# Masking by TensorE in the last attention steps of a two-layer network, with a new order of the work

## The chip, the core and the metric

The kernel runs on one core of a Trainium2 chip. Its time is the device time of one execution in microseconds. Before the change three runs took 934.36, 934.62 and 934.98 us, with a median of 934.62.

The core has five engines, each with its own queue that runs in order: TensorE (PE; its weight loads are listed apart as PEld), VectorE (DVE), ScalarE (ACT), GpSimd (POOL) and SyncE (SP, which starts DMAs here).

## The reference

`x` has 16 batches of 256 rows of 128 features. Everything is fp32.

```python
x = x + 0.5 * L0_ffn(layernorm(x))      # first feed-forward
x = x + L0_attn(layernorm(x))           # linear attention, no softmax
x = x + 0.5 * L0_ffn(layernorm(x))      # second feed-forward, the same weights
x = x + 0.5 * L1_ffn(layernorm(x))      # low-rank experts, 2 of 8 for each batch
x = x + L1_attn(layernorm(x))           # 16 heads of 8, rotary, causal softmax
x = x + 0.5 * L1_ffn(layernorm(x))      # the experts again

# L0_ffn: h = silu(x W1) * (x W2); h = gelu(h H1); h = gelu(h H2); out = h W3   (128 -> 512 -> 512 -> 512 -> 128)
# L1_attn:
scores = einsum('bhqd,bhkd->bhqk', q, k) / sqrt(8)
scores = where(causal, scores, -inf)
attn = softmax(scores, axis=-1)
out = einsum('bhqk,bhkd->bhqd', attn, v)
```

## The kernel before

**Groups and steps.** The 16 batches go in nine groups, seven of two batches (512 rows) and two of one (256 rows). Groups count from 0 to 8, batches from 0 to 15, so groups 7 and 8 are batches 14 and 15. Each group goes through `ffn` twice, 18 times in all. Between the two stands `nonlocal_attn`; after the second come `experts`, `attention` and `after_attention`, which also writes the output.

**A planner writes the order.** Each piece of work is a Python generator, a "line", that yields steps. A step names its engine, an assumed time, how many PSUM banks it takes, which buffers it takes and gives back, and what it needs. The loop at the end of the function always issues the step that the planner's own clocks say can start first; among steps that can start within `SLACK`, it prefers by a key. The line `main` runs the feed-forwards. `HURRY` says how many feed-forwards at the end are preferred to other lines; `PATIENCE` delays an exp when another activation table is loaded; `LOAN` makes the four low banks dearer for short uses; `LATE` is the number of last groups whose attention goes in halves. Assumed times only shape the order. The chip then runs each queue as it was written, with semaphores between engines. Nearly every instruction is recorded by one helper, so the profile gives them all as L227, and tiles tell them apart:

- `xnT`: normalised rows turned round, the input of `w1T` and `w2T`; `sil`: silu of the first product; `h`: hidden rows; `T` and `hS`: sums for a seven-product scheme of the two hidden layers; `w3s`: the last linear's weights
- `qkv`: masked and rotated queries and keys; `mx`: maxima of scores; `pr`: probabilities; `vm`: values; `den`, `rec`, `inv`, `oT`: denominators, their inverses and the scaled output; `wo`: the output projection
- `ab`: an expert's gathered weights; `we`: the merged expert of a batch
- `pb`: the eight PSUM banks

**Attention of one batch.** `maxima` computes scores with queries along the partitions, masks them and reduces them to a maximum for each query and head. Variant 0 and variant 1 are two sets of heads. The negated maxima are turned round (`ident,mx`) and put into spare rows of the queries (`qm`). `weighted` then computes the scores again, transposed, in four quarters `j` in the order 0, 2, 1, 3, each of which takes four banks; `softmax` takes exp of a quarter on ACT, and POOL sets the weights of later keys to zero on the two diagonal blocks, one `affine_select` each. `values` multiplies a quarter by `vm`. In the last `LATE` groups the two variants go one after the other through maxima, quarters, output and a projection each; in the earlier groups they go together.

**Masks.** The flag `ended` is set when the last feed-forward has been issued. From then on the scores of `maxima` are masked by TensorE, which adds `tri` (bf16, from `causal`, -1e30 at later keys) through a bf16 identity `eye` into the bank ahead of the scores; both lie in the tile `wgT`. Before, DVE adds `causal`. From `ended` on, `awake` also issues matmuls of `ident` with `ident` into a free bank wherever the planner sees TensorE idle.

**TensorE's modes.** Most matmuls use the whole array. Scores use four row tiles of 32 x 128 (`tiles="row"`), values four column tiles of 128 x 32 (`tiles="col"`).

Of the kernel before, what the change touches and what calls it, by code (L numbers as in the profile page):

```python
# [20 lines left out]
P = 128  # L21
# [7 lines left out]
LOAN = 1.5  # L29
SPARED = 0.5  # L30
PATIENCE = 1.5
HURRY = 1
# [11 lines left out]
LATE = 2  # L44
SPLIT = 0
HID = 512
KC = HID // P
# [10 lines left out]
def macaron_kernel(ctx: ExitStack, tc: tile.TileContext, a: dict, out: bass.AP):  # L58
# [316 lines left out]
    def ffn(which, t0, n):  # L375
# [79 lines left out]
        for c in range(KC):  # L455
            r = yield pe(0.215 * n, banks=1, after=0.0, take=("h",) if c == 0 else ())
            h = r[1] if c == 0 else h
            pu = r[0]
            nc.tensor.matmul(pu.t[:, :N], w1T[:, c * P : (c + 1) * P], xnT.t[:, :N], start=True, stop=True)
            sil = sml.tile([P, TG], F32, name="sil", bufs=3)  # L460
            spawn(silu(c, pu, sil))
            (pw,) = yield pe(0.215 * n, banks=1, after=0.0, drop=(xnT,) if c == KC - 1 else ())
            nc.tensor.matmul(pw.t[:, :N], w2T[:, c * P : (c + 1) * P], xnT.t[:, :N], start=True, stop=True)
            spawn(product(c, pw, sil, h))
            if me == (0, 0) and c == 1:
                fold_w3()
        lo, hi = 0, 2 * P
        for l, w in ((1, h1T), (2, h2T)):
# [9 lines left out]
            for p, b, first, at, second, needs in (  # L478
# [9 lines left out]
                for o in range(2):  # L488
                    for k in range(2):
                        begins, ends = o + k == 0, o + k == 2  # L490
                        drop = ()
                        if ends and p in (5, 7, 4):
                            drop = (T[{5: 1, 7: 3, 4: 4}[p]],) + ((h,) if p == 4 else ())
                        r = yield pe(
                            0.1075 * n, banks=int(new and begins), after=0.0, take=("h",) if p == 1 and begins else (),
                            needs=needs, drop=drop, sets=(("P6", l, me),) if p == 6 and ends else (),
                        )
                        if new and begins:
                            bk[b] = r[0]
                        if p == 1 and begins:  # L500
                            nh = r[1]
                        src = block(h, *second) if type(second) is tuple else T[second].t[:, :, :M]
                        nc.tensor.matmul(
                            in_two(bk[b])[:, o, :], first[:, k, at + o * P : at + o * P + P], src[:, k, :],
                            start=new and begins, stop=p in (2, 3, 4, 6) and k == 1, skip_group_check=True,
                        )
# [12 lines left out]
            h = nh  # L519

        half = n // 2
        po = {}
        up, down = (0, 1, 2, 3), (2, 3, 0, 1)
        for t, ks in [(t, down) for t in range(half, n)] + [(t, up) for t in range(half)]:
            new = t in (0, half)
            last = t in (half - 1, n - 1)
            r = yield pe(
                0.225 * len(ks), banks=int(new), after=0.0, needs=tuple((2, i, t // half, me) for i in range(2)),
                drop=(h,) if t == half - 1 else (),
            )  # L530
            if new:
                po[t // half] = r[0]
            b = po[t // half]
            for k in ks:
                nc.tensor.matmul(
                    b.t[:, t % half * P : (t % half + 1) * P], h.t[:, k, t * P : (t + 1) * P], w3s[:, k, :],
                    start=(k == ks[0]), stop=(k == ks[-1]),
                )
            if last:
                spawn(residual(t // half, b))  # L540
# [11 lines left out]
    def nonlocal_attn(t0, n):  # L552
# [20 lines left out]
        gram = yield from product(0.45 * nb, None, None, "gram", (xn,))  # L573
        m = yield from product(0.22 * nb, gram, pht, "gph")
        m = yield from product(0.22 * nb, m, wgT, "eff")
        if t0 == 2 * FIRST[NG - 1]:
            spawn(for_the_mask())
        (po,) = yield pe(0.45 * nb, banks=1, drop=(xnT,))
# [8 lines left out]
    def gated(nb, cls):  # L587

        (bk,) = yield pe(0.22 * nb, banks=1)
# [35 lines left out]
        (bk,) = yield pe(0.23 * nb, banks=1, drop=(ab,))  # L625
# [12 lines left out]
    def applied(key, sg, xnT):  # L638
        yield step(None, 0.0, needs=(key,))
        we = merged[key]  # L640
        (po,) = yield pe(0.225 * sg.n, banks=1, drop=(we, xnT) if sg.last else (xnT,))
# [61 lines left out]
    def attention(sg):  # L703
# [6 lines left out]
        if sg.first:  # L710

            (bk,) = yield pe(0.22 * nb, banks=1)
# [35 lines left out]
        (bk,) = yield pe(0.225 * n, banks=1, needs=(("q", sg.t0),), drop=(xnT,))  # L748
# [76 lines left out]
        def weighted(i):  # L825
# [10 lines left out]
            def softmax(j, q, pr):  # L836

                yield act(4 * o - 96, table="exp", drop=(q,))
                nc.scalar.activation(pr[:, :, :o], q.t[:, :, :o], AF.Exp)
                yield step("POOL", 0.65 * sum(k == f for k, f, _ in runs), sets=(("pr", sg.t0, i, j),))  # L840
# [40 lines left out]
            def values():  # L881

                po = [None, None]
                for j in (0, 2, 1, 3):
                    new = j == 0 or (late and j == 1)
                    yield step(None, 0.0, needs=(("pr", sg.t0, i, j), ("v", sg.t0)))
                    pr = prs[j]
                    r = yield pe(0.025 + 0.00174 * o, banks=int(new), tiles="col", drop=(pr,))
                    if new:
                        po[j % 2 :] = [r[0]] * (2 - j % 2)  # L890
                    half = slice((j % 2) * w, (j % 2) * w + w)
                    pp = po[j % 2].t[:, half]
                    for k, f, at in runs:
                        for r in range(4):
                            nc.tensor.matmul(
                                pp[32 * r : 32 * r + 32, (f - q0) * P :], vm.t[:, base // P + k, r, j, :],
                                pr.t[:, r, at : at + (q1 - f) * P],
                                start=(j < 2 and k == 0), stop=(j >= 2 and k == q1 - 1), skip_group_check=True,
                            )
                    if late and j >= 2:  # L900
                        spawn(output(pp, oT[:, half], w // 32, j % 2, po[j % 2], ("oT", sg.t0, i, j)))
                    elif j == 3:
                        spawn(output(po[0].t[:, : 2 * w], oT[:, : 2 * w], w // 16, 0, po[0], ("oT", sg.t0, i, j)))
# [3 lines left out]
            for j in (0, 2, 1, 3):  # L907
                q, prs[j] = yield pe(
                    0.11 + 0.00174 * o, banks=4, tiles="row", take=("pr",), needs=(("qm", sg.t0, i, j % 2),), after=0.0
                )  # L910
                for k, f, at in runs:
                    for r in range(4):
# [3 lines left out]
                            qm[rows, j % 2, base + f * P : base + q1 * P], start=True, stop=True,  # L916
                        )
                spawn(softmax(j, q, prs[j].t))
# [189 lines left out]
    def feed_forwards():  # L1108

        for which, sg in order:  # L1110
# [13 lines left out]
            if (which, sg) == order[0]:  # L1124
                fold_rest()
        ended[0] = True
# [10 lines left out]
    while lines:  # L1137
# [5 lines left out]
        line = min(soon, key=lambda r: ((r[2] is main) == back, r[2].rank, r[1]))[2]  # L1143
# [72 lines left out]
```

## Time and profile before

| | us |
|---|---|
| median of the runs | 934.62 |
| the profiled execution | 934.55 |
| its span, first to last instruction | 932.8 |
| TensorE busy | 904.2 |
| VectorE busy | 636.3 |
| ScalarE busy | 471.5, of which table loads (86 in the group, 1283 ns each) 110.3 |
| GpSimd busy | 356.4, of which 128 selects of `pr` 78.8 |

The span is 1.75 us shorter than the time of the same execution. "Busy" is the time in which an engine runs at least one instruction. Matmuls overlap, so a group's mean duration is longer than the distance between the starts of two neighbours; the prediction goes by starts. A row of the timeline gives start, duration, engine, line, operation, tile written and tiles read, form and count, and, in brackets, how long the engine was idle before and what ended that. A row of the windows gives start and end, length, then the busy time and count of PE, PEld, DVE, ACT and POOL, the granted share of TensorE's clock, the DMA share and GB/s.

### The profile page before, as it was taken

What the parts mean: (1) busy time and instruction counts of PE and PEld (TensorE: products, weight loads), DVE (VectorE), ACT (ScalarE), POOL (GpSimd) and SP (SyncE); (2) the same over time, 40 slices, a digit from 0 to 9 for tenths busy, and PEclk for the clock granted to TensorE, in tenths of its full rate; (3) what the DMA queues carried; (4) which work ended last, traced back from release to release, by engine and by line L of the source; (5) the groups of instructions that cost most, each with busy time, mean ns of one, the idle gap of its engine ahead of it and who ended that gap; (6) DMA issues with size and microseconds to landing.
All of it is one profiled execution on the core that took longest, in us unless ns stands there. A gap on an engine that the chain in (4) does not pass through costs nothing.

```text
span 932.8 us, 16458 instructions
## 1 busy us (share of the span) xinstructions
PE 904.2 (97%) x6524; PEld 680.5 (73%) x6524; DVE 636.3 (68%) x1474; ACT 471.5 (51%) x691; POOL 356.4 (38%) x537
## 2 busy tenths in 40 slices
PE   6999999999999999999999999999999989999998
PEld 4778778686786767787677767866786767877666
DVE  4744646875488485894678764894778586977773
ACT  2233533645754646546555466547574657465332
POOL 5311313522454334442453324532463246443441
PEclk9999999999999999999999999999999999999999
DMA  8100000000000000000000000000000000000000
GB/s 240 33 1 1 1 1 12 12 1 1 13 12 12 1 2 12 24 1 1 12 1 24 1 1 13 24 1 1 13 2 23 1 12 1 25 7 2 13 19 12
DMA packets 14588, 13.68 MB, mean 15 GB/s; under 512 B 2032, under 2 KB 11952, under 8 KB 14512
## 3 DMA queue, kind: packets, MB, share of 16 engines
q1 hardware_dynamic: 12496, 8.04, 3.0%
q0 software_dynamic: 1600, 4.20, 1.6%
q8 instruction: 51, 0.84, 0.4%
q10 hardware_dynamic: 416, 0.39, 0.1%
q14 instruction: 25, 0.20, 0.1%
HBM read 10.53 MB, written 2.10 MB: 14 GB/s over the span
## 4 chain that ended last, share of the span: by engine, by line
PE 70%; DVE 14%; ACT 6%; issue 4%; POOL 2%; DMA 2%; SPq 1%; POOLq 0%; DVEq 0%
PE pb L227 70%; DVE mx L227 4%; DVE h L227 3%; ACT L227 2%; ACT pr L227 2%; DVE pb L227 2%; DMA w3s<-in_w3T_dram 1%; ACT h L227 1%; POOL pr L227 1%; DVE T L227 1%; DMA x<-in_x_dram 1%; DVE st L227 1%; DVE qkv L227 1%; POOL rstd L227 1%; DVE row L227 0%
## 5 line engine op out<-in xcount | busy, mean ns | idle before, releaser
L227 DVE TENSOR_TENSOR h<-h,pb 128x512 f32<-128x512 f32 (+1 forms) x180 | 111.7, 620 | 80.8 <-PE pb L227 78.8
L227 PE MATMUL pb<-T,hS 128*128 128x256 f32 (+1 forms) x576 | 131.8, 364 | 3.9 <-DVE h L227 2.8
L227 POOL TENSOR_SCALAR_AFFINE_SELECT pr<-pr 128x512 f32<-128x512 f32 x128 | 78.8, 639 | 140.4 <-ACT pr L227 135.3
L227 ACT ACTIVATE h<-h 128x512 f32<-128x512 f32 (+1 forms) x108 | 62.3, 581 | 137.7 <-DVE h L227 137.3
L227 ACT ACTIVATE pr<-pb 128x1536 f32<-128x1536 f32 x64 | 92.7, 1449 | 54.0 <-PE pb L227 40.4
L227 PE MATMUL pb<-qkv 32*128 32x256 f32 (+2 forms) x1536 | 115.2, 406 | 4.7 <-ACT pr L227 2.5
L227 ACT ACT_TABLE_LOAD x86 | 110.3, 1283 | 17.8 <-PE pb L227 15.5
L227 DVE TENSOR_REDUCE mx<-pb 128x8 f32<-128x2048 f32 (+1 forms) x64 | 111.9, 1750 | 6.1 <-PE pb L227 5.7
L227 PEld LDWEIGHTS pb<-T,hS 128*128 128x128 f32 x576 | 96.5, 190 | 21.1 <-issue 8.6
L227 DVE TENSOR_TENSOR pb<-pb,causal 128x1024 f32<-128x1024 f32 x56 | 68.7, 1226 | 45.4 <-PE pb L227 37.3
L227 PEld LDWEIGHTS pb<-qkv 32*128 32x128 f32 x1536 | 68.0, 184 | 38.3 <-issue 11.4
L227 ACT ACTIVATE xn<-x,shift,rstd 128x128 f32<-128x128 f32 x138 | 57.1, 482 | 52.9 <-POOL shift L227 52.7
L227 POOL TENSOR_SCALAR nm<-mv 128x4 f32<-128x4 f32 (+3 forms) x56 | 14.8, 264 | 168.3 <-DVE mv L227 167.1
L227 POOL TENSOR_TENSOR T<-h 128x512 f32<-128x512 f32 (+1 forms) x48 | 53.4, 1112 | 58.9 <-ACT h L227 54.9
L227 POOL TENSOR_TENSOR T<-h,T 128x512 f32<-128x512 f32 (+1 forms) x40 | 46.1, 1151 | 64.9 <-DVE h L227 35.0
L227 PE MATMUL pb<-xnT,w1T 128*128 128x512 f32 (+1 forms) x144 | 68.9, 560 | 0.9 <-ACT xnT L227 0.9
L227 PE MATMUL pb<-xnT,w2T 128*128 128x512 f32 (+1 forms) x144 | 68.2, 555 | 1.0 <-ACT sil L227 0.8
L227 PE MATMUL pb<-h,h1T 128*128 128x256 f32 (+1 forms) x288 | 68.8, 364 | 0.0
L227 POOL TENSOR_TENSOR rstd<-ve,mhalf 128x4 f32<-128x4 f32 (+3 forms) x63 | 58.9, 935 | 24.9 <-DVE ve L227 20.1
L227 PE MATMUL pb<-h,h2T 128*128 128x256 f32 (+1 forms) x288 | 67.1, 364 | 0.0
L227 PE MATMUL pb<-T,h1T 128*128 128x256 f32 (+1 forms) x288 | 66.1, 359 | 0.0
L227 PEld LDWEIGHTS pb<-w3s,h 128*128 128x128 f32 x512 | 60.6, 192 | 7.0 <-issue 6.0
(138 smaller groups left out, 1568.9 us busy)
## 6 DMA issues: line engine op xcount, KB each, us to landing
out_dram<-x SPq DMA_DIRECT2D x7, 256.0 KB, 2.3
x<-in_x_dram SPq DMA_DIRECT2D x6, 256.0 KB, 5.3
h1T<-in_h1T_dram SPq DMA_DIRECT2D x1, 1024.0 KB, 9.6
h2T<-in_h2T_dram SPq DMA_DIRECT2D x1, 1024.0 KB, 11.0
ab<-in_eab_dram,at POOLq DMA_INDIRECT x32, 2.9
x<-in_x_dram SPq DMA_DIRECT2D x3, 128.0 KB, 5.4
w1T<-in_w1T_dram SPq DMA_DIRECT2D x1, 256.0 KB, 3.5
w2T<-in_w2T_dram ACTq DMA_DIRECT2D x1, 256.0 KB, 3.9
```

The costliest lines, as they stand in the source:

```text
L227: return lambda *args, **kw: tc.keep_in_program_order(getattr(self.engine, name)(*args, **kw))
```

## The change

1. **Planner constants.** `LOAN` 1.5 to 1.0, `PATIENCE` 1.5 to 1, `HURRY` 1 to 0, `LATE` 2 to 3. The assumed times of many TensorE steps grow by 0.015 us or about 5%.
2. **Last linear.** The part of `ffn` that multiplies by `w3s` becomes a generator of its own, spawned as a line. `main` ends the feed-forwards with a step that needs the last feed-forward's two residuals, and sets `ended` after it.
3. **Mask of the transposed scores.** In `weighted`, where `ended` is set, eight bf16 matmuls (`tri` as the stationary operand, `eye` moving, 128 columns) put the mask into the diagonal blocks of a quarter ahead of its scores; `softmax` then issues no select for it.
4. **Values.** Where a group isn't in the last `LATE`, two quarters (0 and 2, then 1 and 3) go in one step.
5. **Choice among ready steps.** While TensorE is in a tile mode, a ready step with tiles goes ahead of one without.

```diff
-LOAN = 1.5
+LOAN = 1.0
...
-PATIENCE = 1.5
-HURRY = 1
+PATIENCE = 1
+HURRY = 0
...
-LATE = 2
+LATE = 3
...
-            r = yield pe(0.215 * n, banks=1, after=0.0, take=("h",) if c == 0 else ())
+            r = yield pe(0.015 + 0.215 * n, banks=1, after=0.0, take=("h",) if c == 0 else ())
...
-        half = n // 2
-        po = {}
...
+        def last_linear(h=h):
+
+            half = n // 2
+            po = {}
...
+                if last:
+                    spawn(residual(t // half, b))
+
+        spawn(last_linear(), since=0.0)
...
-            def softmax(j, q, pr):
-
-                yield act(4 * o - 96, table="exp", drop=(q,))
+            def softmax(j, q, pr, masked):
+
+                yield act(4 * o - 96, table="exp", drop=(q,), sets=(("pr", sg.t0, i, j),) if masked else ())
                 nc.scalar.activation(pr[:, :, :o], q.t[:, :, :o], AF.Exp)
+                if masked:
+                    return
                 yield step("POOL", 0.65 * sum(k == f for k, f, _ in runs), sets=(("pr", sg.t0, i, j),))
...
-                for j in (0, 2, 1, 3):
-                    new = j == 0 or (late and j == 1)
-                    yield step(None, 0.0, needs=(("pr", sg.t0, i, j), ("v", sg.t0)))
...
+                for js in ((0,), (2,), (1,), (3,)) if late else ((0, 2), (1, 3)):
+                    new = js[0] == 0 or (late and js[0] == 1)
+                    yield step(None, 0.0, needs=tuple(("pr", sg.t0, i, j) for j in js) + (("v", sg.t0),))
+                    r = yield pe(
+                        (0.025 + 0.00174 * o) * len(js), banks=int(new), tiles="col", drop=tuple(prs[j] for j in js)
+                    )
...
+                masked = ended[0]
                 q, prs[j] = yield pe(
-                    0.11 + 0.00174 * o, banks=4, tiles="row", take=("pr",), needs=(("qm", sg.t0, i, j % 2),), after=0.0
+                    0.11 + 0.00174 * o + (0.75 if masked else 0.0), banks=4, tiles="row", take=("pr",),
+                    needs=(("qm", sg.t0, i, j % 2),), after=0.0,
                 )
+                if masked:
+                    diagonal = [at for k, f, at in runs if k == f]
+                    for r in range(4):
+                        for at in diagonal:
+                            nc.tensor.matmul(
+                                q.t[:, r, at : at + P], tri, eye, start=at == diagonal[0], stop=False, skip_group_check=True
+                            )
...
+        yield step(None, 0.0, needs=tuple(("ffn", h, (1, order[-1][1].t0)) for h in range(2)))
         ended[0] = True
...
         back = engine == "PE" and begun[0] <= len(order) - HURRY
-        line = min(soon, key=lambda r: ((r[2] is main) == back, r[2].rank, r[1]))[2]
+        inside = engine == "PE" and tiles[0] is not None
+        line = min(
+            soon, key=lambda r: (inside and r[2].next["tiles"] is None, (r[2] is main) == back, r[2].rank, r[1])
+        )[2]
```

## The prediction

> **What bounds the kernel now.** First the page's busy times, then the same by stretch of the span.
>
> ```profile
> span 932.8 us, 16458 instructions
> PE 904.2 (97%) x6524; PEld 680.5 (73%) x6524; DVE 636.3 (68%) x1474; ACT 471.5 (51%) x691; POOL 356.4 (38%) x537
> ```
>
> ```profile
> 400.00:500.00 100.00, 99.82 (x722) 74.45 (x720) 68.01 (x144) 54.12 (x72) 38.35 (x53) 1.00 0.03 9
> 750.00:800.00 50.00, 45.86 (x423) 36.30 (x421) 39.46 (x113) 31.08 (x48) 28.42 (x44) 1.00 0.03 8
> 850.00:875.00 25.00, 23.45 (x259) 17.11 (x260) 19.71 (x52) 9.59 (x14) 10.33 (x16) 1.00 0.04 12
> 875.00:900.00 25.00, 23.61 (x254) 16.80 (x252) 21.52 (x62) 8.50 (x11) 10.91 (x17) 1.00 0.06 17
> 900.00:933.00 33.00, 26.21 (x267) 19.42 (x264) 14.38 (x35) 6.95 (x7) 6.33 (x10) 0.94 0.03 9
> ```
>
> From about 30 to 600 us TensorE all but never stops: what is put on it or taken from it there is paid in full. After 850 its busy time deceives. Of the 100 matmuls of `ident` with `ident`, 90 are fillers that `awake` puts there; at 0.22 us each 19.8 us of the last 83 are no work. The end is a chain of latencies, read from the timeline:
>
> ```profile
> 843.47 2.05 PE L227 MATMUL pb<-w3s,h 128*128 128x128 f32 x16
> 869.08 0.60 PE L227 MATMUL pb<-wgT 128*128 128x256 bf16 x4
> 895.48 0.61 PE L227 MATMUL pb<-wgT 128*128 128x256 bf16 x4
> ```
>
> The last linear of the last feed-forward ends at 845.4. Batch 14 starts its first masked score at 869.1, batch 15 at 895.4, the end is 932.8: sections A, B, C of 23.7, 26.3 and 37.4, together 87.4 us. [...]
>
> **The change part by part.** A host planner writes the order, so new cost constants reorder everything. I took counts from the built order of both kernels and priced them by the trace.
>
> *Mode changes.* [...]
>
> ```profile
> 809.57 1.95 PE L227 MATMUL pb<-T,hS 128*128 128x128 f32 x16
> 811.35 0.83 PE L227 MATMUL pb<-h,h2T 128*128 128x128 f32 x6
> 834.99 1.95 PE L227 MATMUL pb<-T,hS 128*128 128x128 f32 x16
> 836.87 0.94 PE L227 MATMUL pb<-qkv 32*128 32x256 f32 x16
> ```
>
> Sixteen equal passes took 1.78 us ahead of the same mode and 1.88 ahead of row tiles. Over all starts of the trace the median pass of 128 columns is 112 ns, and 205 ahead of another mode; of 256 columns 216 and 309. One change costs 93 ns. The two-quarter step and the preference for tile lines take them from 378 to 332: 46 x 0.093 = 4.3 us less. The Trainium skill ("TensorEngine Tiling (Array Packing)", Key Properties) says that a change of mode drains the array, without a price; its fixed part of an isolated warm matmul, 166 ns ("TensorE: Matmul & The Clock Gate", Single matmul latency), would make 7.6 us by estimate. The row decides: 4.3.
>
> *Work added.* `LATE` 3 sends the two batches of group 6 the split way: 4 more transposes of maxima and 4 more projections by `wo`, 8 x 0.22 = 1.8 us of TensorE; on DVE 4 halves of den, rec, inv and oT in place of 2 wholes, (4 x 1.56) - (2 x 2.42) = 1.4 us, hidden under TensorE. The masks are 64 bf16 matmuls of 128 columns, each with a weight load. The trace has only 256 columns, at 108 ns from start to start.
>
> ```profile
> L227 PEld LDWEIGHTS <-wgT 128*128 128x128 bf16 x32 | 3.1, 97 | 1.8 <-issue 1.5
> ```
>
> Half of 108 is 54, the load alone 97, both in turn 151. I take 97, the time of the one part that the trace shows in just this form: 6.2 us (3.5 to 9.7). All stand after the last linear, where they partly replace fillers (90 to 63, -5.9 us).
>
> *Work removed.* Only 16 of 128 selects go, those of batches 14 and 15; group 6 keeps its own. A pair costs 1.22 us on POOL between exp and values.
>
> *Table loads.* The smaller `PATIENCE` lets exp cut in sooner: 87 loads become 111.
>
> ```profile
> 839.32 1.45 ACT L227 ACTIVATE pr<-pb 128x1536 f32<-128x1536 f32 x1
> 840.79 1.28 ACT L227 ACT_TABLE_LOAD   x1
> 842.08 0.38 ACT L227 ACTIVATE h<-pb 128x256 f32<-128x256 f32 x1
> ```
>
> Exp ends at 840.77, the load runs 840.79 to 842.07, the next activation starts 0.01 later: 1.28 us all told, 24 x 1.283 = 30.8 us more ACT, from 51% to 54% busy. The skill speaks harder against the change here ("ScalarE: Activation LUTs", What ACT_TABLE_LOAD costs): a drain of about 1.38 us comes with each load, 2.66 in all. That would be 63.8 us, and ACT at 57%. The rows show no such drain; I take 30.8, hidden while TensorE has other lines to run. Uncovered, every microsecond is paid: the first rival below.
>
> *What moves.* With `HURRY` 0 the feed-forward yields to every other ready line to its very end; the last linear, now its own line, may also use the low banks. In the built order the work of TensorE ahead of the last `w3s` matmul, fillers and changes left out, priced at 429, 216 and 112 ns a pass (two passes for fp32, tiles four at a time), grows from 756.2 to 764.4 us. Behind it, it falls from 37.1 to 30.7. Ahead there are 31 changes fewer (2.8 us). The last linear therefore ends 8.2 - 2.8 = 5.4 us later if the idle time ahead stays: 850.8. That is a choice. Between the end of the third last linear (742.0) and of the last (845.2) there are 103.2 us for 88.0 of work, so 15.2 idle; after there are 95.3 of work. Idle of 5 (all but the hops filled) to 26 (as thinly covered as ACT's new loads allow) bounds it: -10 to +11 us.
>
> *Section A, 23.7 to 8.6.* The queries of batch 14 come before or just behind the last linear, no longer 13 us later. The way to its first masked score runs along ACT: from 0.5 us ahead of the linear's end a table load 1.28, three remaining exps 3 x 1.45, between them y 0.49, keys and query 4 x 0.59, xnT 0.37, then a hop of 0.1: -0.5 + 1.28 + 4.35 + 3.2 + 0.1 = 8.4, taken as 8.6. Before, six exps lay behind the linear, each with a select.
>
> *Section B, 26.3 to 31.4.* With batch 14's first masked score as zero: scores and reduces of the first variant end at 7.2 (1.9, 2.29, 1.5, 1.22, hops), the second variant's large reduce at 12.8. The masks of the first quarter wait for the bank that `we` of batch 15 reads last, 10.5; exp ends 13.5. Second quarter: masks, scores 14.1 to 15.8, exp to 17.4. Values, transposes and the expert product of batch 15: 18.2. Its residual, norm, POOL's rstd 0.72 and xn: 21.6. Third exp ends 22.5, fourth quarter's masks and scores 24.1, its exp 25.75, its values 26.6. Only behind them stand `wqk` of batch 15 (27.6); rotary on DVE and POOL, and the last query 3.8 more. This order costs 5.1 us.
>
> *Section C, 37.4 to 35.3.* What it is now:
>
> ```profile
> 918.76 1.45 ACT L227 ACTIVATE pr<-pb 128x1536 f32<-128x1536 f32 x1 [1.26 <-PE pb L227]
> 920.28 1.22 POOL L227 TENSOR_SCALAR_AFFINE_SELECT pr<-pr 128x512 f32<-128x512 f32 x2 [1.49 <-ACT pr L227]
> 921.28 0.59 PEld L227 LDWEIGHTS pb<-pr,vm 128*32 128x32 f32 x16
> ```
>
> The last values start 25.9 after the section's start. Afterwards: first quarter's masks 8 x 0.097 on the way, exp at 11.2 in place of 10.2; second quarter ready when that exp ends (12.6), its exp to 16.4, values 17.4; third masks and scores 19.1, exp 20.8; the fourth's last four masks wait for that exp, scores 22.1, exp 22.3 to 23.7, values at 23.8. The select and its hop are gone (1.3), three masks lie on the path, an earlier second quarter makes up for them: -2.1. The rest, 11.5 us, is unchanged.
>
> *Sum.* 8.6 + 31.4 + 35.3 = 75.3 against 87.4: -12.1. With +5.4: 932.8 - 6.7 = 926.1 span. The profiled run took 934.55, 1.75 around its span: 927.9. The median before, 934.62, is 0.07 above: **928.0 us**. If masks cost 54 or 151, some 40 on the path shift it by about -2 or +2.
>
> **The rivals.**
>
> *ACT starves the feed-forward (slower).* One of the loads added is between silu and exp in the last feed-forward, where TensorE has few other lines; in the stretch to the last linear ACT's sum by the trace's means goes from 36 us to 50, beside 63 of TensorE, 13 loads in place of 9. If each of the four more costs its load and the exp that it brings, 4 x (1.28 + 1.45) = 10.9 us of idle TensorE: 938.9. Against it: ACT's waits for DVE (137.3 us for h) show slack all along, and no wait of matmuls on sil passes 1 us now. It decides from 6.7 us, 22% of the 30.8.
>
> *The shorter end is eaten (no change).* DVE is busy 41.2 of 50 us from 850 to 900. If A and B are DVE's, the end shrinks by just the 5.4 that moved ahead: 934.6. For it: reduces of 2.29 us. Against it: 17 us less DVE work by the means lies behind the last linear.
>
> *The idle time ahead is filled (faster).* `HURRY` 0 exists in the order: attention matmuls stand between those of the last feed-forward. If 8 of 15.2 idle go: 920.0.
>
> **How the numbers follow.** My forecast 0.55, own range 922 to 932; filled idle 0.17; eaten 0.10; starved 0.18. The bound of 0.2% (1.9 us) is what a measurement can tell from no change: faster 0.55 + 0.17 = 0.72, same 0.10, slower 0.18. The range 917 to 940 reaches from below the filled case to above the starved one, with the masks' two ends.
>
> **What would show it.** Right: last `w3s` pass ending near 851; batch 14's first mask some 9 us later, batch 15's 31 after that; values following exp by 0.1 us; a pass ahead of a mode change still 93 ns longer, 46 fewer. Wrong: the linear's end past 858 with matmuls waiting on sil or ACT h; section A over 15 us; mask pairs above 151 ns; gaps of TensorE between 100 and 600 us, where there are none now.

## The result: 0.8% slower, and the profile after

The kernel after takes 941.59 us (median, 939.11 to 944.07) against 934.36 of the kernel before, a ratio of 1.0076 with an interval of 1.0059 to 1.0093. The forecast was 928.0. The profiled execution took 944.07 us, 1.7 around its span. It is the slowest of the five, so some 2.5 us of what its profile shows belong to that execution and not to the change. It also had the lowest granted clock of TensorE, 0.991 of full speed, against 0.998 in the execution of 939.11 us. At 0.995 the kernel after took 941.28 to 941.95 us and the kernel before, in all sessions, 934.6 to 935.5, so the loss is there at the same clock. First the page:

```profile
span 942.4 us, 16522 instructions
PE 903.1 (96%) x6546; PEld 682.5 (72%) x6546; DVE 652.3 (69%) x1478; ACT 503.7 (53%) x719; POOL 340.7 (36%) x521
```

TensorE is busy for as long as before (904.2) in a span that is 9.6 us longer, although its fillers fell from 90 to 63 (5.9 us). Most of the loss is idle time of TensorE. One of the windows that the prediction showed, now after (start and end, length, busy us and count of PE, PEld, DVE, ACT, POOL, granted clock, DMA share, GB/s):

```profile
400.00:500.00 100.00, 97.11 (x691) 72.12 (x684) 68.42 (x159) 61.72 (x85) 39.76 (x59) 1.00 0.02 6
```

From 400 to 500 us TensorE rests 2.9 us where it rested 0.2. That is the stretch which the prediction treated as full. The end, read from the timeline:

```profile
868.99 2.05 PE L227 MATMUL pb<-w3s,h 128*128 128x128 f32 x16
878.17 0.60 PE L227 MATMUL pb<-wgT 128*128 128x256 bf16 x4
907.94 0.60 PE L227 MATMUL pb<-wgT 128*128 128x256 bf16 x4
```

From here on I cut each run at two points, read from the starts of the `w3s` groups in its timeline: the 448th of the 512 starts (742.0 before), and the last one (845.2 before; 870.8 after, in the 16 matmuls of the row above). The prediction and the expectations call the first point the end of the third last linear. That is a misreading. The last three linears have 16 starts each, and the point is the end of the first half of the fourth last, that of group 6 (32 starts, from 740.3 to 745.6 before). It is the same point in every run, so the differences stand. Up to it is the *middle*, between the two the *last stages*, behind the second the *tail*. The three lengths are those of the profiled execution; the median and the ratio are of all.

| us | middle | last stages | tail | median | ratio to before, interval |
|---|---|---|---|---|---|
| before | 742.0 | 103.2 | 87.6 | 934.36 | |
| after | 758.0 | 112.8 | 71.6 | 941.59 | 1.0076, 1.0059 to 1.0093 |
| e1 mask alone | 742.2 | 104.6 | 89.1 | 936.51 | 1.0013, 1.0004 to 1.0022 |
| e2 two quarters alone | 737.6 | 106.9 | 91.8 | 937.18 | 1.0021, 1.0013 to 1.0029 |
| e3 own line alone | 754.2 | 108.1 | 92.9 | 957.65 | 1.0228, 1.0200 to 1.0256 |
| e4 larger times alone | 754.1 | 121.0 | 79.6 | 955.21 | 1.0202, 1.0173 to 1.0232 |
| e5 before, no table loads | 739.7 | 102.8 | 86.1 | 931.23 | 0.9958, 0.9942 to 0.9973 |
| e6 after, no table loads | 752.9 | 111.1 | 71.2 | 936.27 | 1.0006, 0.9992 to 1.0021 |
| e7 before, no DVE masks | 741.5 | 100.3 | 85.5 | 929.04 | 0.9935, 0.9913 to 0.9957 |
| e8 after, no DVE masks | 755.8 | 109.6 | 71.6 | 936.69 | 1.0017, 1.0007 to 1.0027 |
| e9 after without e3, e4 | 740.1 | 117.2 | 74.9 | 934.21 | 0.9989, 0.9980 to 0.9998 |
| e10 edits of the end alone | 742.1 | 110.2 | 80.1 | 933.67 | 0.9985, 0.9977 to 0.9992 |
| e11 after without e3 | 762.3 | 117.2 | 74.8 | 955.32 | 1.0205, 1.0180 to 1.0231 |
| e12 after without e4 | 751.0 | 115.4 | 81.9 | 950.22 | 1.0160, 1.0139 to 1.0182 |
| e13 before, constant operands | 742.8 | 104.2 | 88.0 | 935.96 | 1.0000, 0.9991 to 1.0008 |
| e14 after, constant operands | 759.2 | 112.1 | 71.6 | 944.41 | 1.0094, 1.0077 to 1.0110 |
| e15 e3 and e4 at the end only | 740.3 | 112.0 | 82.1 | 937.46 | 1.0019, 1.0012 to 1.0027 |
| e16 before, times 0.9% smaller | 768.0 | 106.4 | 90.9 | 965.02 | 1.0307, 1.0290 to 1.0325 |
| e17 before, cut loose | 746.1 | 102.9 | 86.4 | 935.75 | 1.0003, 0.9993 to 1.0012 |
| e18 after, cut loose | 767.5 | 111.6 | 72.0 | 951.95 | 1.0173, 1.0156 to 1.0190 |

The change made the tail 16.0 us shorter, the last stages 9.6 longer and the middle 16.0 longer. The middle has to be explained. Summed windows from 200 us to the first point, before and then after:

```profile
sum 542.00, PE 538.81 PEld 395.64 DVE 378.05 ACT 302.68 POOL 213.28; mean PE 89.80 PEld 65.94 DVE 63.01 ACT 50.45 POOL 35.55
```

```profile
200.00:300.00 100.00, 97.45 (x690) 70.58 (x689) 75.87 (x158) 56.97 (x77) 35.48 (x54) 0.98 0.03 9
300.00:400.00 100.00, 96.91 (x697) 72.32 (x695) 64.26 (x143) 57.34 (x74) 37.23 (x52) 0.98 0.03 9
...
sum 558.00, PE 543.53 PEld 402.21 DVE 397.26 ACT 326.13 POOL 208.38; mean PE 90.59 PEld 67.04 DVE 66.21 ACT 54.35 POOL 34.73
```

Before, TensorE rests 542.0 - 538.8 = 3.2 us; after, 558.0 - 543.5 = 14.5. That is 11.3 of the 16. The clock is 0.98 in two of the windows, where it was 1.00: twice TensorE was granted half its clock for 3.4 us (rows in the last section), which makes 2 x 3.4 x 0.5 = 3.4 us more.

### The profile page after: what moved, and what is told of

Read it like the earlier page. It is cut to its first block, busy times and chain, and to the rows that moved or that the text cites. A ratio compares the mean times of both kernels' runs of the same rounds, so it can differ in the third digit from the quotient of the medians.

```text
span 942.4 us, 16522 instructions
## 1 busy us (share of the span) xinstructions
PE 903.1 (96%) x6546; PEld 682.5 (72%) x6546; DVE 652.3 (69%) x1478; ACT 503.7 (53%) x719; POOL 340.7 (36%) x521
## 4 chain that ended last, share of the span: by engine, by line
PE 67%; DVE 14%; ACT 8%; issue 6%; POOL 3%; SPq 1%; DMA 0%; POOLq 0%; DVEq 0%; ACTq 0%
PE pb L227 67%; ACT L227 3%; DVE mx L227 3%; ACT pr L227 3%; DVE h L227 2%; DVE pb L227 2%; DVE T L227 1%; ACT h L227 1%; DVE xn L227 1%; DVE rot L227 1%; POOL rstd L227 1%; ACT xn L227 1%; ACT sil L227 0%; DVE den L227 0%; POOL pr L227 0%
## 5 line engine op out<-in xcount | busy, mean ns | idle before, releaser
L227 ACT ACT_TABLE_LOAD x110 | 141.1, 1283 | 14.3 <-PE pb L227 7.8
L227 PE MATMUL pb<-T,hS 128*128 128x256 f32 (+1 forms) x576 | 129.7, 365 | 8.7 <-DVE h L227 5.3
L227 POOL TENSOR_SCALAR_AFFINE_SELECT pr<-pr 128x512 f32<-128x512 f32 x112 | 71.3, 660 | 149.5 <-ACT pr L227 149.3
L227 PEld LDWEIGHTS pb<-qkv 32*128 32x128 f32 x1536 | 68.0, 183 | 44.9 <-ACT pr L227 13.2
L227 DVE TENSOR_TENSOR x<-x,pb 128x256 f32<-128x256 f32 (+2 forms) x79 | 37.4, 474 | 63.9 <-PE pb L227 63.6
L227 ACT ACTIVATE xn<-x,shift,rstd 128x128 f32<-128x128 f32 x128 | 52.9, 482 | 48.6 <-POOL shift L227 48.6
L227 POOL TENSOR_TENSOR T<-h 128x512 f32<-128x512 f32 (+1 forms) x42 | 48.4, 1152 | 80.0 <-ACT h L227 43.1
L227 PE MATMUL pb<-T,h2T 128*128 128x256 f32 (+1 forms) x288 | 66.2, 361 | 0.2 <-POOL T L227 0.2
```

The lines of the kernel that those rows point to most:

```text
L227: return lambda *args, **kw: tc.keep_in_program_order(getattr(self.engine, name)(*args, **kw))
```

## The experiments

**The parts alone.** Four single edits, each cut out of the change and put into the kernel before. Mask of the transposed scores:

```diff
+                masked = ended[0]
...
+                            nc.tensor.matmul(
+                                q.t[:, r, at : at + P], tri, eye, start=at == diagonal[0], stop=False, skip_group_check=True
+                            )
```

> The kernel before with the mask of the transposed scores by TensorE alone (edit 3); the order of the work is otherwise that of before. Theory 1 (added table loads leave TensorE idle) and theory 2 (the new order puts the feed-forward's sums on DVE behind attention's reduces) both expect nothing ahead of the last linear and a small effect behind it: 16 selects fewer, masks in their place, 932 to 936 us. If the masks themselves are the loss, 939 to 942.

Values of two quarters in one step:

```diff
-                for j in (0, 2, 1, 3):
+                for js in ((0,), (2,), (1,), (3,)) if late else ((0, 2), (1, 3)):
```

> The kernel before with two quarters of values in one step alone (edit 4). Mode changes fall by 6.2 us by the trace's 93 ns each, table loads rise from 87 to 106. Theory 1, at 0.65 us of idle TensorE for each added load (16 us more time ahead of the third last linear over 24 loads in the changed kernel): 934.4 - 6.2 + 12.4 = about 940. Theory 2, if this edit keeps the sums on DVE in time: about 928 to 930; if it is the edit that makes them late, above 940 with few table loads at the idle places.

Last linear as its own line:

```diff
+        def last_linear(h=h):
...
+        spawn(last_linear(), since=0.0)
```

> The kernel before with the last linear as its own line alone (edit 2). Table loads 87 to 102, mode changes 1.3 us less. Theory 1: 934.4 - 1.3 + 9.8 = about 943. Theory 2: the sums of each second feed-forward stand behind the work of the next group, so idle time ahead of T,hS matmuls in every second stage, 938 to 944; without that, 933.

Larger assumed times of TensorE:

```diff
-            r = yield pe(0.215 * n, banks=1, after=0.0, take=("h",) if c == 0 else ())
+            r = yield pe(0.015 + 0.215 * n, banks=1, after=0.0, take=("h",) if c == 0 else ())
...
-                            0.1075 * n, banks=int(new and begins), after=0.0, take=("h",) if p == 1 and begins else (),
+                            0.015 + 0.1075 * n, banks=int(new and begins), after=0.0, take=("h",) if p == 1 and begins else (),
```

> The kernel before with the planner's larger assumed times of TensorE alone. Table loads 87 to 99, mode changes 1.9 us less. Theory 1: 934.4 - 1.9 + 7.8 = about 940. Theory 2 expects a loss only if DVE's sums come late: 936 to 940 with idle time ahead of T,hS matmuls; else 932.

The masks alone cost 1.3 thousandths, all behind the middle. The two quarters take 4.4 us out of the middle (6.2 were expected from fewer changes of mode) and lose them and 3.5 more behind it. The two edits that add no work cost the most: 22 us for the own line, 20 for the larger times, with 12 us in the middle for each. The order differs there and what follows from it: table loads (102 and 99) and, at the end, fillers and a few masks that pass from DVE to TensorE. The clock is not needed for this loss. The larger times alone (e4), from 200 us to the first point, in one window:

```profile
200.00:754.00 554.00, 543.36 (x3853) 396.97 (x3853) 399.26 (x859) 305.09 (x421) 209.15 (x308) 1.00 0.03 8
```

TensorE rests 10.6 us in it at a granted clock of 1.00.

**Table loads.** In the orders written, the smaller `PATIENCE` alone gives 87 loads, as before; the own line alone 102, the two quarters 106, the larger times 99. The trace of after has 110 where 86 were:

```profile
L227 ACT ACT_TABLE_LOAD x110 | 141.1, 1283 | 14.3 <-PE pb L227 7.8
```

To see what they cost, both kernels with one function in place of silu and gelu, that needs no other table than exp does; the profile then has a single load, at the start:

```diff
-            nc.scalar.activation(sil[:, :N], pu.t[:, :N], AF.Silu, scale=s1[:, c : c + 1])
+            nc.scalar.activation(sil[:, :N], pu.t[:, :N], AF.Tanh, scale=s1[:, c : c + 1])
...
-            nc.scalar.activation(to, src, AF.Gelu)
+            nc.scalar.activation(to, src, AF.Tanh)
```

> The kernel before with Tanh in place of Silu and Gelu, so that one table serves all and 86 table loads go (110 us of ACT); the order of the work is unchanged and the output is another function's. Both theories: little is to be had, since its loads are covered; 926 to 934 us.

> The changed kernel with Tanh in place of Silu and Gelu: 110 loads (141 us of ACT) go, the order stays. Theory 1 (the 24 added loads are what TensorE waits for): the loss of 7 us turns into the gain that was forecast, 6 us or more below the same edit of the kernel before. Theory 2 (DVE's queue): still 4 us or more above that kernel.

All loads together are worth 4 us in the kernel before and 5 to 7 in the kernel after (by the ratios, 0.42% and 0.70%). Without any, the kernel after is still 936.27 - 931.23 = 5.0 us behind (7.2 with them) and its middle 13.2 us longer (16.0 with them). So the theory that the added loads starve TensorE falls: at most 2 to 3 us are theirs.

**VectorE's load.** TensorE's new waits name DVE most often, so the 56 adds of `causal` by DVE, 1.23 us each, were taken out of both kernels:

```diff
-                    nc.vector.tensor_tensor(
-                        d, d, causal.unsqueeze(1).unsqueeze(1).to_broadcast([P, 4, 2, P]), ALU.add
-                    )
```

> The kernel before without DVE's 56 causal adds ahead of the maxima (68.7 us of DVE; the maxima are then taken over later keys too); the order stays. Theory 1: no change, 933 to 935. Theory 2: few of its sums come late, so 3 to 6 us less at most, mostly behind 750 us: 929 to 932.

> The changed kernel without the same 56 adds on DVE; the order and all 110 table loads stay. Theory 1: 940 to 942, no change. Theory 2: the sums h and the norms xn no longer stand behind them, 10 us or more less, 925 to 931, and the idle time ahead of T,hS between 200 and 700 us is gone for the most part.

Both get 5 to 6 us faster and the distance stays: 7.7 us, in the middle 14.3. A tenth of DVE's work less (56 x 1.23 = 69 of 652 us) leaves the loss as it is. (These two kernels take the maxima over later keys too. By algebra a larger shift cancels in the softmax as long as no exp underflows. Whether one does is open; e7 is the fastest kernel here.)

**The order.** What is left is which instruction stands behind which. Groups in the page, first of before, then of after (busy us, mean ns, then idle time ahead and who ended it):

```profile
L227 PE MATMUL pb<-T,hS 128*128 128x256 f32 (+1 forms) x576 | 131.8, 364 | 3.9 <-DVE h L227 2.8
```

```profile
L227 PE MATMUL pb<-T,hS 128*128 128x256 f32 (+1 forms) x576 | 129.7, 365 | 8.7 <-DVE h L227 5.3
```

The timeline of after shows where such a wait comes from:

```profile
468.20 1.45 ACT L227 ACTIVATE pr<-pb 128x1536 f32<-128x1536 f32 x1
...
469.72 1.62 POOL L227 TENSOR_SCALAR_AFFINE_SELECT pr<-pr 128x512 f32<-128x512 f32 x2 [2.82 <-ACT pr L227]
...
471.30 1.51 PE L227 MATMUL pb<-pr,vm 128*32 128x256 f32 x32
472.74 1.56 PE L227 MATMUL pb<-T,hS 128*128 128x256 f32 x6
472.88 0.72 DVE L227 STREAM_TRANSPOSE den<-pb 128x512 f32<-128x512 f32 x1 [2.61 <-PE pb L227]
473.63 0.35 DVE L227 RECIPROCAL rec<-den 128x32 f32<-128x32 f32 x1
...
474.02 0.71 DVE L227 STREAM_TRANSPOSE inv<-rec 128x512 f32<-128x512 f32 x1
474.65 0.65 DVE L227 TENSOR_TENSOR h<-h,pb 128x512 f32<-128x512 f32 x1
...
475.36 1.99 PE L227 MATMUL pb<-T,hS 128*128 128x256 f32 x8 [1.05 <-DVE h L227]
```

Two quarters' values start as POOL's second select ends. DVE's next instruction is `den`, so DVE stands still for 2.61 us until those values are there. Only behind `den`, `rec` and `inv` comes the sum `h`, and TensorE stands for 1.05 us in front of a product that waits for DVE at that sum. In the kernel before, the same batch's `den` (the sixth in either trace) also stands ahead of the sum. But DVE has other work ahead of it, a residual with its norm, and the sum comes next, ahead of `rec` and `inv`; no row has a bracket for idle time:

```profile
473.74 0.36 DVE L227 BATCH_NORM_AGGREGATE mv<-st 128x2 f32<-128x6 f32 x4
474.02 0.68 DVE L227 STREAM_TRANSPOSE den<-pb 128x512 f32<-128x512 f32 x1
474.62 0.65 DVE L227 TENSOR_TENSOR h<-h,pb 128x512 f32<-128x512 f32 x1
475.20 0.67 DVE L227 TENSOR_TENSOR T<-h 128x512 f32<-128x512 f32 x1
475.79 0.34 DVE L227 RECIPROCAL rec<-den 128x32 f32<-128x32 f32 x1
```

DVE's idle time ahead of `den` and `rec` in the middle of after; before has none there (its 7.7 us are all in the tail):

```profile
its engine sat idle before it (us, times) until:
  PE pb L227: 4.3, 3
```

So waits like this one can be a part of the 11.3 us at most. By name, TensorE waits 5.2 us for DVE's `h` in the middle of after (0.7 before) and 2.1 for its `mx` (0.5).

So my next theory was the order: queues that run in order hold each other up where a consumer stands too soon behind its producer. If so, giving up the two edits that only reorder must give back the middle. The last linear is back in `main` and the assumed times are the old ones:

```diff
-        spawn(last_linear(), since=0.0)
...
-            r = yield pe(0.015 + 0.215 * n, banks=1, after=0.0, take=("h",) if c == 0 else ())
+            r = yield pe(0.215 * n, banks=1, after=0.0, take=("h",) if c == 0 else ())
```

> All edits except two: the last linear stays inside main, and the planner's assumed TensorE times stay as before. In the order written, the work of TensorE ahead of the last w3s matmul is 788.9 us (790.0 with all edits), behind it 31.5 (30.7), and 108 tables are loaded (111). Theory 'order' (these two edits put dependent matmuls close behind their producers all through the middle): the steady stages alternate 51.6 and 55.5 us as with the paired values alone, the third last linear ends near 738 to 743 us in place of 758.0, the end keeps its shorter form (71 to 77 us), TensorE's stalls over 150 ns between 100 and 740 us fall from 21 to below 15 us, and the run takes 922 to 931 us, faster than before. Theory 'the edits of the end cost the time themselves' (masks, changed preference, smaller PATIENCE): third last linear 752 to 760, the run 936 to 943. Theory 'table loads': 108 in place of 111, so no change either, 938 to 942.

The middle comes back whole: 740.1 against 758.0, with 540.0 - 534.7 = 5.3 us of rest in it:

```profile
sum 540.00, PE 534.73 PEld 398.78 DVE 384.09 ACT 325.85 POOL 204.78; mean PE 89.12 PEld 66.46 DVE 64.02 ACT 54.31 POOL 34.13
```

This shows that, with all other edits in place, the 16 us come with these two (and with 107 table loads in this trace, once more that they don't hang on the loads). But the run did not reach the 922 to 931 that I expected: the last stages take 14 us more than before, and the tail's 12.7 go there. Which of the two edits is it, in company of the others?

```diff
-        spawn(last_linear(), since=0.0)
```

> All edits except the last linear as its own line. 107 table loads. Theory 'order', if either of the two edits is enough to bring the dependent matmuls close behind their producers: third last linear 752 to 760, the run 936 to 945. If the last linear's own line is what did it (alone it cost 21 us): third last linear near 742, the run 924 to 932. Theory 'the edits of the end': 936 to 943.

```diff
-            r = yield pe(0.015 + 0.215 * n, banks=1, after=0.0, take=("h",) if c == 0 else ())
+            r = yield pe(0.215 * n, banks=1, after=0.0, take=("h",) if c == 0 else ())
```

> All edits except the planner's larger assumed TensorE times. 109 table loads. Theory 'order', if either edit is enough: third last linear 752 to 762, the run 936 to 948. If the larger assumed times are what did it (alone they cost 19 us): third last linear near 742, the run 924 to 932. Theory 'the edits of the end': 936 to 943.

Either is enough to lengthen the middle (762.3 and 751.0), and each without the other makes a slower kernel than both: 955 and 950 us. The costs of edits don't add up here; each makes another order. Is it anything about these two? The kernel before, with assumed times of the feed-forward that are 0.9% smaller:

```diff
-            r = yield pe(0.215 * n, banks=1, after=0.0, take=("h",) if c == 0 else ())
+            r = yield pe(0.2130 * n, banks=1, after=0.0, take=("h",) if c == 0 else ())
...
-                            0.1075 * n, banks=int(new and begins), after=0.0, take=("h",) if p == 1 and begins else (),
+                            0.1065 * n, banks=int(new and begins), after=0.0, take=("h",) if p == 1 and begins else (),
...
-                0.225 * len(ks), banks=int(new), after=0.0, needs=tuple((2, i, t // half, me) for i in range(2)),
+                0.2230 * len(ks), banks=int(new), after=0.0, needs=tuple((2, i, t // half, me) for i in range(2)),
```

> The kernel before with the feed-forward's assumed TensorE times 0.9% smaller (0.213, 0.1065 and 0.223 in place of 0.215, 0.1075 and 0.225), nothing else; the same instructions in another order (104 table loads in place of 87). If any shift of the planner's clocks disturbs the middle, as the two edits did: third last linear 748 to 762, the run 940 to 957. If it is these two edits in particular (work put in more often, larger times): third last linear 740 to 745, the run 931 to 937.

It need not be these two. This meaningless shift costs 29.6 us beside the 935.45 of before in the same runs, 26.0 in the middle, more than the change itself, with 104 table loads. It is one shift of one size, so how the costs of such shifts spread is not known. The waits are others than in after. TensorE waits 7.8 us for `mx` in the middle and 3.7 for `h`, and DVE's idle time ahead of `den` and `rec` is twice as long there:

```profile
its engine sat idle before it (us, times) until:
  PE pb L227: 8.2, 4
```

**Is it one kind of wait?** The waits named most are those of the feed-forward's products. In both kernels its matmuls were given a constant in place of what they read, with the order kept, so that they wait for PSUM banks alone:

```diff
-            nc.tensor.matmul(pu.t[:, :N], w1T[:, c * P : (c + 1) * P], xnT.t[:, :N], start=True, stop=True)
+            nc.tensor.matmul(pu.t[:, :N], w1T[:, c * P : (c + 1) * P], w1T[:, :N], start=True, stop=True)
...
-                        src = block(h, *second) if type(second) is tuple else T[second].t[:, :, :M]
+                        src = w1T[:, :N].rearrange("p (k m) -> p k m", k=2)
```

> The kernel before, but every matmul of the feed-forwards (w1T, w2T, the fourteen products of the two hidden layers, w3s) reads a constant part of w1T in place of xnT, h, T and hidden rows; so the feed-forward's TensorE work has the same instructions in the same order and waits for no data, only for PSUM banks. The feed-forward's values are thus left out of the result. Both theories: TensorE's stalls between 100 and 742 us are 7.6 us before, of which some 4 are of the feed-forward or follow from it, so the third last linear ends 735 to 742 us (before 742.0).

> The kernel after with the same substitution: the feed-forward's matmuls wait for no data, in the same order as after. Theory 'in-order waits' (TensorE stands in front of matmuls of the feed-forward whose DVE or ACT producer is late, and DVE in front of work that waits for those): the third last linear ends within 4 us of the same point in the kernel before with this substitution, so 737 to 746 us in place of 758.0, and stalls over 150 ns between 100 and 742 us fall from 21 to below 12 us. Rival 'the loss is not in the feed-forward's waits' (the other lines' waits for banks, maxima and probabilities, or the clock): still 10 to 16 us later than that kernel, 748 to 758.

No gain in either: the middle of after ends at 759.2, where the theory that these matmuls wait for their data wanted 737 to 746. At the place shown above, TensorE stood even longer:

```profile
470.91 1.51 PE L227 MATMUL pb<-pr,vm 128*32 128x256 f32 x32
...
474.00 0.72 DVE L227 STREAM_TRANSPOSE den<-pb 128x512 f32<-128x512 f32 x1 [4.12 <-PE pb L227]
...
475.77 0.65 DVE L227 TENSOR_TENSOR h<-h,pb 128x512 f32<-128x512 f32 x1
...
476.48 0.70 PE L227 MATMUL pb<-w1T,hS 128*128 128x256 f32 x2 [2.56 <-DVE h L227]
```

A product that reads nothing that DVE writes here still waits for DVE's sum. What is left for it to need is the PSUM bank, which the sum reads. (`den` starts 1.6 us after the end of the values here, 0.1 in after. It starts just behind the six products that follow the values, which end at 473.91. The same is so in e8, whose edit is not at this place: there the six end at 472.62 and `den` starts at 472.69. I have no explanation for that; it makes this place of e14 worse than in after.) So the same again, where DVE and ACT don't read the feed-forward's banks either:

```diff
-                h.t[:, c, :N], pw.t[:, :N], s2[:, c : c + 1], sil[:, :N], ALU.mult, ALU.mult
+                h.t[:, c, :N], w1T[:, :N], s2[:, c : c + 1], sil[:, :N], ALU.mult, ALU.mult
...
-            copy(block(nh, 1, 1), in_two(a))
+            copy(block(nh, 1, 1), still)
```

> The kernel before with TensorE's feed-forward work cut loose in both directions: its matmuls read a constant (as in e13), and silu, gelu, the products h and the sums of the hidden layers read a constant too, in place of the PSUM banks of pb that the matmuls write. Same order; the feed-forward's values are left out of the result. So no matmul of the feed-forward waits for a bank that DVE or ACT still has to read, except the last linear's, which the residual still reads. Both theories: stalls of the feed-forward's matmuls were about 1.5 us in e13, so the third last linear ends between 738 and 743 us (e13: 742.8).

> The kernel after, cut loose in the same way. Theory 'banks' (what holds TensorE in the middle are PSUM banks that DVE reads late; e14 showed that they are not the data): of the 22.1 us of stalls in e14 some 10 are of the feed-forward's matmuls, which now have nothing to wait for, so the third last linear ends 8 to 13 us earlier than in e14 (759.2), at 746 to 751, and its distance to the kernel before with the same cut falls from 16.4 to 3 to 9 us. Rival 'it is the order as a whole' (one wait taken away comes back as another, at the maxima, the normalised rows or the router): still 12 to 17 us behind that kernel, 753 to 759.

My theory of the banks finds no support either. The distance in the middle is 767.5 - 746.1 = 21.4 us, not 3 to 9. But e18 is 10 us slower than after and its late `den` is still there, so it is no clean test. TensorE now runs through the products at this place and stands a few matmuls later, for the same length, at the projection behind the same chain:

```profile
475.30 1.51 PE L227 MATMUL pb<-pr,vm 128*32 128x256 f32 x32
...
476.74 3.29 PE L227 MATMUL pb<-w1T,hS 128*128 128x256 f32 x14
...
478.35 0.72 DVE L227 STREAM_TRANSPOSE den<-pb 128x512 f32<-128x512 f32 x1 [4.09 <-remote]
...
482.61 0.71 PE L227 MATMUL pb<-wo,oT 128*128 128x128 f32 x4 [2.58 <-POOL oT L227]
```

So no single kind of wait that I took away carries the loss. At the one place that I followed, the wait came back at the next instruction of TensorE that needs the late chain exp, selects, values, `den`, `inv`, `oT`. That the other waits do the same is not shown, and neither is how much each chain is late. What is shown is that the order makes the loss; which pairs of instructions stand too close in it stays open.

**The end by itself.** Three edits that leave the middle's order as it was:

```diff
-HURRY = 1
+HURRY = 0
...
-LATE = 2
+LATE = 3
...
+                masked = ended[0]
```

> Only three edits: mask of the transposed scores by TensorE, HURRY 0 and LATE 3. In the order written, the stages up to the third last linear are as before; the work of TensorE ahead of the last linear is 789.2 us (before 784.7), behind it 35.2 (before 37.1), 90 table loads (87). Theory 'order': third last linear at 742 +- 1 us, the tail 74 to 81, the last linear 845 to 851, the run 925 to 932. Theory 'the edits of the end cost the time': the end gives nothing when the middle is left alone, so 934 to 940.

And all edits, with the own line and the larger times only from the last but one feed-forward on:

```diff
-        spawn(last_linear(), since=0.0)
+        if begun[0] > len(order) - 2:
+            spawn(last_linear(), since=0.0)
+        else:
+            yield from last_linear()
```

> All edits, but the last linear's own line and the larger assumed times hold only from the last but one feed-forward on. In the order written, the stages up to the third last linear are those of e9; ahead of the last linear lie 785.8 us of TensorE work (after 790.0), behind it 33.9 (30.7). Theory 'order' (the two edits cost only where they disturb the middle): third last linear 740 +- 2, the last three stages 184 to 191 (after 184.3, e9 192.2), so the run 925 to 933. Rival (the end is no shorter, what leaves the tail goes ahead of it): last three stages 191 to 196, the run 933 to 937.

With only the end's edits the middle is untouched (742.1), the tail 7.5 us shorter and the last stages 7.0 longer: 933.67 us, 1.5 thousandths faster than before and the best of the kernels that keep the reference's functions and all of its masks. In e15 the middle is at 740.3 and the last stages with the tail take 194.1 us, 3.3 more than before. The expectation that 184 to 191 would come out of it missed.

## Why the prediction was wrong, step by step

*Mode changes.* Right. Over the starts of the trace a pass of 256 columns takes 216 ns, and 309 ahead of another mode, as forecast. In the traces, some records of which are missing, the changes fall from 342 to 301, so 41 x 0.093 = 3.8 us against 4.3.

*Work added.* Right in kind, too large for the masks:

```profile
887.64 0.62 PE L227 MATMUL pb<-wgT 128*128 128x128 bf16 x8
888.20 0.94 PE L227 MATMUL pb<-qkv 32*128 32x256 f32 x16
```

Eight masks take 0.56 us to the start of the scores, where 8 x 0.097 = 0.78 was taken: 56 ns from start to start, with the change of mode in the last one (149). The weight loads, 97 ns each by their records, add nothing to that. That is the lower end of what I had left open, 3.6 us in place of 6.2.

*Work removed.* Right: 112 selects remain, 16 fewer.

*Table loads.* The count and the price were right: 24 more, ACT 503.7 against 471.5 us busy, +32.2 for the 30.8 forecast. "Taken as hidden" was nearly right: e5 and e6 leave 2 to 3 us. The cause I gave was wrong: `PATIENCE` alone adds none, and the single edits e2, e3 and e4 each add 12 to 19 without it.

*What moves.* This is the step that failed: the last linear "ends 8.2 - 2.8 = 5.4 us later if the idle time ahead stays". Its last matmul starts at 870.8 in place of 845.2, 25.6 us later. I looked at idle time only in the last stages. There the choice held: 112.8 - 95.3 = 17.5 us of idle against 15.2. But 16.0 us came from the middle, 11.3 of them new rests of TensorE and 3.4 two stretches at half clock. There the forecast had no term but "TensorE all but never stops", which is a statement about the old order. I carried it over to an order that was new throughout, although I had written that new constants reorder everything. The last sign that I named for "wrong", gaps of TensorE between 100 and 600 us, is what came.

*Sections.* Section A ended 7.4 us after the linear's last start (8.6 forecast), B 29.8 (31.4), C 34.5 (35.3). Together 71.6 against 75.3: the part that was worked out most closely was right, and 3.7 us too careful, of which the masks are some 2 by the prediction's own estimate.

*The sum.* The forecast's span of 926.1, with 870.8 - 850.8 = 20.0 for the later linear and -3.7 for the sections, gives 942.4, the span of the profiled execution. So the linear's start is the whole miss.

*Rivals.* "ACT starves the feed-forward" named 938.9, close to the result, by the wrong road: e6 has no table loads and loses 5.0 of the 7.2 us. "The shorter end is eaten" fits e10 in its number, for the edits of the end: 7.5 out of the tail, 7.0 back ahead of it. That DVE does it, as that rival said, is not shown. "The idle time ahead is filled" is refuted. No rival was "the new order is worse in the stretch that was full", which was the case. Its sign at least was to be had: with 0.2 us of rest in 100, a new order could only add idle time there.

## What to carry to other kernels

Where a planner writes the order, a change of its constants or the splitting off of a line is a change of the whole schedule. In a stretch where the bounding engine never stops, a new order can only add idle time, so that time needs a term of its own, or the edit must be confined to the part that it is for. Test first what an equally small, meaningless shift of the constants does: here the one that I tried, 0.9%, cost 29.6 us, more than any edit was meant to gain. And where one wait is removed and the time stays, follow the chain that was late to the next instruction that needs it, before naming the cause.

## What the runs showed of the hardware

The granted clock of TensorE falls to one half for some 3.4 us at a time. It did so twice in the middle of after, and both times a stretch with rests of TensorE lay ahead (0.79 of 3.30 and 1.44 of 3.50 us):

```profile
267.50:270.80 3.30, 2.51 (x15) 1.98 (x15) 2.79 (x4) 1.50 (x3) 3.22 (x3) 1.00 0.00 0
270.80:274.20 3.40, 3.40 (x14) 3.04 (x13) 3.08 (x12) 2.34 (x5) 1.35 (x2) 0.50 0.29 82
352.60:356.10 3.50, 2.06 (x18) 1.14 (x20) 2.05 (x6) 2.80 (x3) 1.23 (x2) 1.00 0.00 0
356.10:359.50 3.40, 3.40 (x34) 1.89 (x27) 3.03 (x13) 0.29 (x1) 1.41 (x2) 0.51 0.00 0
```

But rests alone don't do it. In e12 TensorE rested 2.24 of 3.50 us, and the clock stayed full:

```profile
459.50:463.00 3.50, 1.26 (x6) 0.76 (x4) 3.50 (x6) 1.40 (x2) 2.05 (x2) 1.00 0.20 69
463.00:466.50 3.50, 2.56 (x12) 2.01 (x13) 3.50 (x5) 0.00 (x0) 0.00 (x0) 1.00 0.02 6
```

What decides between the two is open. The middle of before has no such fall in its profiled execution. The rests cost time without it: e3 and e4 keep a clock of 1.00 there and lose 12 us each.

I had also not expected bf16 masks of 128 columns to follow one another every 56 ns, each with a weight load of 97 ns. It is half of the 109 ns of the masks with 256 columns.
